# A graph attention layer and a mixture of experts on one core: nodes laid out by partition (p * 48 + t) or by tile (t * 128 + p)

## The chip, the core and the metric

The kernel runs on one core of a Trainium2 chip. The metric is the device time of one execution in microseconds (us). PE is TensorE, DVE is VectorE, ACT is ScalarE, POOL is GpSimd, and SP is the SyncE queue that issues most of the transfers.

## The reference

There are 6250 nodes of 256 numbers (`x`) and a sorted list of 100,000 edges, `src` and `dst`. The first layer needs the first 6250 edges only:

```python
xn = layernorm(x)
xt = (xn @ weight).reshape(-1, 4, 64)
alpha_l = einsum('ehd,hd->eh', xt[src], attn_l)
alpha_r = einsum('ehd,hd->eh', xt[dst], attn_r)
alpha = softmax(leaky_relu(alpha_l + alpha_r, 0.01), axis=1)
tmp = einsum('nh,nhd->nd', alpha[:6250], xt[dst[:6250]])   # node n uses edge n
x = x + broadcast of tmp over the 4 heads
```

The second layer takes the layernorm of x as tokens, routes each to its 2 best of 8 experts, and adds their outputs, weighted, to the token; the sum is added to x:

```python
logits = tokens @ router_w.T;  rw, re = top_k(softmax(logits), 2);  rw = rw / rw.sum()
for e in range(8):
    out = out + combine[:, e:e+1] * (gelu(tokens @ w1[e] + b1[e]) @ w2[e] + b2[e])
```

`src` is uniform over the nodes. `dst` is `6250 * u ** 2` for uniform u, truncated to an integer and sorted, so the first 6250 edges name only the lowest-numbered nodes.

## The kernel before

The nodes fill 49 tiles of 128 lanes. Node t * 128 + p lies in tile t on partition p; tile 48 holds the last 106. The program sets the order of every engine's instructions by hand (`manual_schedule`, L133), so an engine takes its instructions in the order in which they are written, and one that waits holds up what stands behind it.

**Loads and lists (L185 to L232).** The edge lists come as rows, 49 x 128, by SP: 48 whole rows, then the last row of 106 (L194, L195). Between the two lists stands the load of the first four tiles of x (L197), after them the other loads of x, up to four tiles each (L206), and the last tile in two pieces (L208). ACT's queue brings the weights, the router and the attention vectors (L198 to L201). The dst list is cast, transposed on PE and cast back to integers (L229 to L232), so that `dst_sb[p, t]` is the edge's target of node t * 128 + p.

**Own terms (L667 to L684).** For each group of up to four tiles of x, PE transposes them (`turn`, L240; ACT copies the result out of PSUM), forms the attention and router terms (`own_terms`, L417, into `own_T`), and turns them back (`back`, L430). DVE takes the mean and variance of 12 or 13 tiles at a time (`statistics`, L402) and scales the terms (`source_end`, L440). Other work is put between these steps by number (`fillers`, L649). Just ahead of this part the src list is split into its low 7 bits (the partition) and the rest (the tile) by DVE (L336 to L350): the partition numbers go through a DRAM tile `highs` to all partitions as `high_1` (L352, L353), which a filler turns into a one-hot table (L655); the tile numbers go through PE to `low`, from which a filler makes `low_0` (L652).

**Gathers (L234, L643).** POOL gathers the rows x[dst] for each tile by an indirect transfer. A small copy on POOL (`pace`, L645) ties the start of every second gather to the progress of the own terms and, later, of the features. A gather is asked for 20 tiles ahead of its use. The 31 middle tiles go to `big`, which later holds the experts' second weights, the other 18 to `xd_own`.

**Features (L755 to L780).** For each gathered tile PE turns it, multiplies with `w_sb` (`features`, L464), and looks up the source terms by matmuls with the two tables (`look_up`, L489); DVE reduces these (L505). Interleaved with the next group of tiles are softmax and weighted sum (`attend_1` to `attend_3`) and routing (`route`, L559), which writes the rows of its group, R = 337 numbers each, to the DRAM table (L593).

**Sorting by expert pair (L783 to L903).** Each token's place among the tokens of its pair of experts is counted by matmuls (`rank`, L605), and a matrix product (L856) gives for each slice and lane the partition and the tile of the token that goes there (`pi`). `held_by` (L901) is its row in the table, and serves as its row of the output too. Then the 125 units (slice and expert) are numbered (L935 to L948), and SP, ACT, PE and DVE load these numbers to registers (`name_units`, loads at L1051).

**Experts (L1125 to L1168).** A pipeline runs over the units: SP loads the first weights (`fill`, L1079), PE multiplies (`first`, L1091; `second`, L1107), ACT applies gelu (L1098), DVE accumulates (L1114). POOL fetches the rows of slices through `held_by` (`fetch`, L914), a token norm is worked off in steps (`norm`, L971), `turn_slice` (L1037, L1038) brings the tokens to `tokT`, and POOL scatters finished slices to the output (`finish`, L1118).

Of the kernel before, what the change touches and what calls it, by code (L numbers as in the profile page):

```python
# [9 lines left out]
FP = mybir.dt.float32  # L10
BF = mybir.dt.bfloat16
I32 = mybir.dt.int32
AF = mybir.ActivationFunctionType
ALU = mybir.AluOpType
# [8 lines left out]
def kernel(  # L23
# [33 lines left out]

    nc = tc.nc  # L60
    N, D = x.shape
    H, OC = attn_l.shape
    NE, _, F = w1.shape
    P = 128
    NT = -(-N // P)
    LAST = N - (NT - 1) * P
    GROUPS = [(0, 10), (10, 10), (20, 9), (29, 10), (39, 10)]
    NG = len(GROUPS)
    GT = max(n for _, n in GROUPS)
# [12 lines left out]
    TS = 128  # L82
    NS = -(-N // TS)
# [15 lines left out]
    HUGE = 2.0**127  # L99
    ROOT_D = D**-0.5  # L100
    assert sum(n for _, n in GROUPS) == NT == NS and HD == D and F == D and NE == 8
    assert 96 <= LAST < P

    const = ctx.enter_context(tc.tile_pool(name="const", bufs=1))
    early = ctx.enter_context(ExitStack())
    held = early.enter_context(tc.tile_pool(name="held", bufs=1))
    ps = ctx.enter_context(tc.tile_pool(name="ps", bufs=2, space=PSUM))
# [20 lines left out]
    number = const.tile([128, 1], FP, name="number")  # L128
    ident = const.tile([128, 128], FP, name="ident")
    ident_b = const.tile([128, 128], BF, name="ident_b")  # L130
    held_by = const.tile([TS, NS], I32, name="held_by")

    dst_sb = held.tile([P, NT], I32, name="dst_sb")  # L133
    xs = [held.tile([P, n, R], FP, name=f"x{g}") for g, (_, n) in enumerate(GROUPS)]
# [39 lines left out]
    small = early.enter_context(tc.tile_pool(name="small", bufs=2))  # L174
# [6 lines left out]
    first_pool = setup.enter_context(tc.tile_pool(name="setup", bufs=1))  # L181
    raw = first_pool.tile([128, DC, HD], FP, name="raw")
    rows = first_pool.tile([NE, D], FP, name="rows")
    att = first_pool.tile([2 * H, OC], FP, name="att")
    edges = [first_pool.tile([NT, P], I32, name=name) for name in ("dst_rows", "src_rows")]  # L185
    whole = (NT - 1) * P
    for of in edges:
        nc.vector.memset(of, 0)

    g_last, n_last = GROUPS[-1]  # L190
    nc.vector.memset(xs[-1][96:, n_last - 1, :D], 0.0)
    x_v = x[0:whole, :].rearrange("(t p) d -> p t d", p=P)
    for of, e in zip(edges, (dst, src)):
        nc.sync.dma_start(of[: NT - 1, :], e[0:whole].rearrange("(t p) -> t p", p=P))  # L194
        nc.sync.dma_start(of[NT - 1 :, :LAST], e[whole:N].rearrange("(t p) -> t p", t=1))  # L195
        if e is dst:
            nc.sync.dma_start(xs[0][:, :4, :D], x_v[:, :4, :])  # L197
    nc.scalar.dma_start(raw, weight.rearrange("(c p) f -> p c f", p=128))  # L198
    nc.scalar.dma_start(rows, router_w)
    for k, a in enumerate((attn_r, attn_l)):  # L200
        nc.scalar.dma_start(att[k * H : (k + 1) * H, :], a)  # L201
    for g, (t0, n) in enumerate(GROUPS):
        for k in range(0, n, 4):
            m = min(4, NT - 1 - t0 - k, n - k)
            if m > 0 and t0 + k > 0:
                nc.sync.dma_start(xs[g][:, k : k + m, :D], x_v[:, t0 + k : t0 + k + m, :])  # L206
# [4 lines left out]
    for of, pattern, k in ((count_up, [[1, 128]], 0), (number, [[0, 1]], 1)):  # L211
        nc.gpsimd.iota(
            of, pattern=pattern, base=0, channel_multiplier=k,
# [9 lines left out]
    nc.vector.memset(counts[:, 0, :], 0.0)  # L223
    nc.vector.tensor_scalar(ident, count_up, number, None, ALU.is_equal)
    nc.vector.tensor_copy(ident_b, ident)


    edge_f = first_pool.tile([NT, P], FP, name="edge_f", bufs=2)
    nc.vector.tensor_copy(edge_f, edges[0])  # L229
    pe = ps.tile([P, NT], FP, name="pe", tag="r")  # L230
    nc.tensor.transpose(pe, edge_f, ident[:NT, :NT])
    nc.vector.tensor_copy(dst_sb, pe)  # L232

    def gather(t):  # L234
        nc.gpsimd.indirect_dma_start(  # L235
# [97 lines left out]
        nc.vector.tensor_copy(w_sb[:, c, AR:MEAN], pa[:, 0, :])  # L333


    parts = []  # L336
    for k, (op, by) in enumerate(
        ((ALU.bitwise_and, P - 1), (ALU.logical_shift_right, P.bit_length() - 1))
    ):
        part = edges[0] if k else first_pool.tile([NT, P], I32, name="src_part")  # L340
        nc.vector.tensor_scalar(part, edges[1], by, None, op)
        parts.append(part)
    high_b = first_pool.tile([NT, P], BF, name="high_b")
    nc.vector.tensor_copy(high_b, parts[0])
    low_f = first_pool.tile([NT, P], FP, name="edge_f", bufs=2)
    nc.vector.tensor_copy(low_f, parts[1])
    pe = ps.tile([P, NT], FP, name="pe", tag="r")
    nc.tensor.transpose(pe, low_f, ident[:NT, :NT])
    low = first_pool.tile([P, NT], BF, name="low")
    nc.vector.tensor_copy(low, pe)  # L350
    highs = dram.tile([1, NT * P], BF, name="highs")
    nc.sync.dma_start(highs.rearrange("o (t p) -> (o t) p", p=P), high_b)  # L352
    nc.sync.dma_start(high_1[:, : NT * P], highs.to_broadcast([P, NT * P]))  # L353
# [199 lines left out]


    table = dram.tile([NT * P, R], FP, name="table")
    table_v = table.rearrange("(t p) r -> p t r", p=P)
    ranks = {}

    def route(g):  # L559
# [195 lines left out]
    at = {}  # L755
    for k, (g, b, n) in enumerate(FEATURES):
        if b == 0:
            at = tasks(g)
        after = None
        for j in range(n):  # L760
            i = b + j
            features(g, i, blocks, j)
            t = GROUPS[g][0] + i
# [20 lines left out]
    n = GROUPS[z][1]  # L784
# [40 lines left out]
    parts = []  # L825
    for k, (op, by) in enumerate(
# [4 lines left out]
        part = small.tile([P, NTE], BF, name=f"part{k}", bufs=1)  # L831
# [11 lines left out]
    for t0, t1 in ((0, 10), (10, 24), (24, NTE)):  # L843
        at, n = slice(t0, t1), t1 - t0
# [16 lines left out]
    for k in range(2):  # L861
# [34 lines left out]
    nc.vector.tensor_tensor(  # L896
        is_unit, long(count_up[:NS, :NU], NE), wide(unit, NU), ALU.is_equal
    )
    tile_of = small.tile([TS, NS], FP, name="tile_of", bufs=1)
    nc.vector.tensor_copy(tile_of, pi[:, 1, :])  # L900
    nc.vector.scalar_tensor_tensor(  # L901
        held_by, tile_of, float(P), pi[:, 0, :], op0=ALU.mult, op1=ALU.add
    )  # L903

    xrs, toks, norms, w1s, hids = ({} for _ in range(5))

# [42 lines left out]

    early.close()
    late = ctx.enter_context(tc.tile_pool(name="late", bufs=3))
    tokT = late.tile([128, NS * D], FP, name="tokT", bufs=1)
# [161 lines left out]
    def finish(s):  # L1116
        n = min(TS, N - s * TS)
        nc.gpsimd.indirect_dma_start(  # L1118
            out=ends_at[s][:, :],
            out_offset=bass.IndirectOffsetOnAxis(ap=held_by[:n, s : s + 1], axis=0),  # L1120
            in_=acc[:n, s * D : (s + 1) * D], in_offset=None,
        )

# [76 lines left out]
```

## Time and profile before

| | us |
|---|---|
| runs of the kernel: median of 3 (lowest, highest) | 430.03 (427.4, 430.1) |
| the profiled execution, its own time | 440.06 |
| its span, first to last instruction | 438.3 |
| PE busy | 376.8 (86%) |
| DVE busy | 311.0 (71%) |
| ACT busy | 225.1 (51%) |
| POOL busy | 201.3 (46%) |

Starts and durations below count from the start of the span of that one profiled execution. A timeline line gives start, duration (of all instructions merged in it), engine, line, operation, out<-in, shape and count, and in brackets the idle time of the engine before it and what ended that. A line of stages gives the stretch, its length, then busy time and count for PE, PE's weight loads, DVE, ACT and POOL, then the granted clock of PE as a share of full speed, the busy share of the 16 DMA engines (over 1 where packets of several queues overlap), and what they moved in GB/s.

### The profile page before, as it was taken

The numbers are of one execution on the slowest core, as the hardware profiler recorded it, in microseconds if no ns is written. First come the engines' busy times: TensorE is split into PE (matmuls) and PEld (weight loads), VectorE is DVE, ScalarE is ACT, GpSimd is POOL, SyncE is SP. The second block draws the span as 40 slices with busy tenths as digits, with TensorE's granted clock in tenths as the row PEclk, the third lists the DMA queues.
The fourth block names the chain that finished last, engine by engine and source line by source line (L and its number), as shares of the span: only waits on it lengthen the run. The fifth ranks groups of instructions, "written<-read, shape, count | busy, mean of one in ns | idle before, by whom it ended". The sixth has DMA issues, their size and how long they took to land.

```text
span 438.3 us, 9881 instructions
## 1 busy us (share of the span) xinstructions
PE 376.8 (86%) x2576; PEld 322.4 (74%) x2576; DVE 311.0 (71%) x1083; ACT 225.1 (51%) x658; POOL 201.3 (46%) x240
## 2 busy tenths in 40 slices
PE   5977979998995018879999999999999999999991
PEld 4745757776884016459999998988988899999990
DVE  5979412989879987548789778777876877655551
ACT  3654457866773100057676666566576577333330
POOL 0077868889222000563443467555665643322222
PEclk9896889999998555699999999999999999999997
DMA  7979544473971340396656676767776666666620
GB/s 239 352 212 84 103 76 80 78 222 117 273 234 59 138 157 0 88 278 167 203 166 203 191 213 203 233 198 207 204 215 201 199 183 192 182 187 196 182 72 22
DMA packets 59109, 74.63 MB, mean 170 GB/s; under 512 B 7171, under 2 KB 54103, under 8 KB 58801
## 3 DMA queue, kind: packets, MB, share of 16 engines
q1 hardware_dynamic: 51504, 52.45, 40.0%
q0 software_dynamic: 7248, 21.29, 20.0%
q8 instruction: 23, 0.38, 0.4%
q10 hardware_dynamic: 304, 0.27, 0.2%
q14 instruction: 30, 0.24, 0.2%
HBM read 59.13 MB, written 14.87 MB: 169 GB/s over the span
## 4 chain that ended last, share of the span: by engine, by line
PE 52%; issue 1%; POOL 1%; ACT 1%; POOLq 0%; ACTq 0%; DVE 0%
PE ph L1091 25%; PE py L1107 24%; PE pt L1037 2%; POOL xr L914 0%; POOLq L1195 0%; ACT tokT L1038 0%; ACT acc L1014 0%; POOL out_dram L1118 0%; ACT tok L1004 0%; POOL nm L994 0%; ACT hid L1098 0%; ACTq L1051 0%; POOL mv L993 0%; ACTq L1098 0%; ACT nm L1010 0%
## 5 line engine op out<-in xcount | busy, mean ns | idle before, releaser
L1091 PEld LDWEIGHTS ph<-tokT,w 128*128 128x128 f32 x1000 | 129.7, 191 | 17.5 <-ACT tokT L1038 5.6
L1091 PE MATMUL ph<-tokT,w 128*128 (+1 forms) x1000 | 133.3, 276 | 5.9 <-ACT tokT L1038 3.3
L1107 PE MATMUL py<-big,hid 128*128 x500 | 128.9, 381 | 0.0
L1098 ACT ACTIVATE hid<-ph,b_cols 128x128 f32<-128x128 f32 x250 | 78.4, 366 | 82.7 <-PE ph L1091 67.2
L1107 PEld LDWEIGHTS py<-big,hid 128*128 128x128 f32 x500 | 85.4, 191 | 7.4 <-DVE acc L1114 0.6
L1114 DVE SCALAR_TENSOR_TENSOR acc<-py,shares,acc 128x256 f32 (+1 forms) x125 | 60.5, 484 | 32.4 <-PE py L1107 15.0
L914 POOL DMA_INDIRECT xr<-table,held_by x49 | 49.3, 1006 | 72.2 <-DVE held_by L901 39.1
L1118 POOL DMA_INDIRECT out_dram<-acc,held_by x49 | 50.9, 1040 | 55.0 <-DVE acc L1114 39.6
L1114 DVE SCALAR_TENSOR_TENSOR acc<-big,shares,acc (+1 forms) x125 | 60.1, 481 | 10.5 <-issue 5.0
L468 PE MATMUL px<-w_sb,tT 128*128 128x293 f32 x196 | 57.4, 423 | 3.8 <-issue 3.3
L1004 ACT ACTIVATE tok<-xr,nm 128x256 f32<-128x256 f32 x49 | 29.5, 603 | 57.2 <-DVE nm L1000 41.1
L468 PEld LDWEIGHTS px<-w_sb,tT 128*128 128x128 f32 x196 | 34.7, 193 | 12.1 <-issue 3.9
L235 POOL DMA_INDIRECT big<-in_x_dram,dst_sb x31 | 34.9, 1126 | 8.1 <-issue 7.4
L250 ACT COPY tT<-pt 128x512 f32<-128x512 f32 (+2 forms) x56 | 27.5, 528 | 13.9 <-PE pt L246 10.5
L476 ACT COPY pxs<-px 128x293 f32<-128x293 f32 x49 | 19.7, 402 | 27.5 <-PE px L468 15.0
L978 DVE TENSOR_TENSOR xr<-xr 128x512 f32<-128x512 f32 (+1 forms) x25 | 17.3, 692 | 17.3 <-issue 17.2
L1014 ACT ACTIVATE acc<-xr,nm 128x256 f32<-128x256 f32 x49 | 29.1, 597 | 0.0
L505 DVE TENSOR_REDUCE ag<-pl 128x8 f32<-128x392 f32 (+1 forms) x25 | 13.8, 551 | 19.3 <-PE pl L501 7.6
L993 POOL TENSOR_SCALAR mv<-mv 128x2 f32<-128x2 f32 (+1 forms) x25 | 5.6, 226 | 38.6 <-DVE mv L990 34.4
L235 POOL DMA_INDIRECT xd_own<-in_x_dram,dst_sb x18 | 19.3, 1073 | 4.9 <-issue 4.1
L246 PE MATMUL pt<-ident,x 128*128 128x128 f32 x98 | 17.1, 324 | 3.8 <-issue 2.0
L497 PE MATMUL pl<-al_sb,high 128*128 128x196 bf16 x147 | 18.6, 246 | 1.8 <-DVE ag L505 1.8
(210 smaller groups left out, 481.3 us busy)
## 6 DMA issues: line engine op xcount, KB each, us to landing
w<-in_L_ffn_w_dram SPq DMA_DIRECT2D x125, 256.0 KB
table<-x SPq DMA_DIRECT2D x4, 1685.0 KB
x<-in_x_dram SPq DMA_DIRECT2D x10, 512.0 KB
big<-in_L_ffn_w_dram SPq DMA_DIRECT2D x2, 1024.0 KB
high<-highs SPq DMA_DIRECT2D x1, 1568.0 KB
table<-x SPq DMA_DIRECT2D x1, 1516.5 KB
big<-in_L_ffn_b_dram SPq DMA_DIRECT2D x1, 1024.0 KB
xr<-table,held_by POOLq DMA_INDIRECT x49
```

The costliest lines, as they stand in the source:

```text
L235: nc.gpsimd.indirect_dma_start(out=xd(t), out_offset=None, in_=x[:, :], in_offset=bass.IndirectOffsetOnAxis(ap=dst_sb[:, t : t + 1], axis=0),)
L250: nc.scalar.copy(tT, pt)
L468: nc.tensor.matmul(px, blocks[c][:, k * P : (k + 1) * P], w_sb[:, c, :], start=(c == 0), stop=(c == DC - 1),)
L476: nc.scalar.copy(pxs[:, i, :], px)
L914: nc.gpsimd.indirect_dma_start(out=xr[:, i, :], out_offset=None, in_=table[:, :], in_offset=bass.IndirectOffsetOnAxis(ap=held_by[:, s0 + i ...
L1004: nc.scalar.activation(tok[:, i, :], xr[:, i, :D], AF.Identity, bias=bias[:, i : i + 1], scale=scale[:, i : i + 1],)
L1014: nc.scalar.activation(acc[:, s * D : (s + 1) * D], xr[:, i, :D], AF.Identity, bias=bias[:, i : i + 1], scale=more[:, i : i + 1],)
L1091: nc.tensor.matmul(ph[:, j, :], w[:, c * F + j * 128 : c * F + (j + 1) * 128], tokT[:, bass.ds(rows_at + c * TS, TS)], start=(c == 0), sto ...
L1098: nc.scalar.activation(hid[:, j, :], ph[:, j, :], AF.Gelu, bias=b1_cols[:, :, j][:, bass.ds(at_act[u][0], 1)])
L1107: nc.tensor.matmul(py, hid[:, j, :], we2[:, j, bass.ds(at_pe[u][1], D)], start=(j == 0), stop=(j == FC - 1),)
L1114: nc.vector.scalar_tensor_tensor(to, y, share, to, op0=ALU.mult, op1=ALU.add)
L1118: nc.gpsimd.indirect_dma_start(out=ends_at[s][:, :], out_offset=bass.IndirectOffsetOnAxis(ap=held_by[:n, s : s + 1], axis=0), in_=acc[:n, ...
```

## The change

With PER = 48 and `whole` = 48 * 128 = 6144, node p * 48 + t (t below 48) lies in tile t on partition p, so that 48 neighbours in x share a partition; the last 106 nodes are tile 48, node `whole` + p on partition p, as before. A load of four tiles of x then takes four consecutive rows for each partition. The table is laid out likewise, row p * 49 + t. The edge lists are loaded straight to their partitions, 48 numbers each; the last 106 edges come as a column by two small loads for each list on ACT's queue. The transposes of the dst list and of the low part of src go. In their place the src list is divided by 48 on DVE (shift by 4, times 171, shift by 9), the remainder and the exception of the last 106 nodes are worked out, and the partition numbers are transposed on PE. As the rows of the table and of the output are no longer numbered alike, `held_out` is worked out by four operations of DVE, called between the unit numbers and the experts.

```diff
-    LAST = N - (NT - 1) * P
+    PER = NT - 1
+    whole = PER * P
+    LAST = N - whole
...
+    held_out = const.tile([TS, NS], I32, name="held_out")
...
-    edges = [first_pool.tile([NT, P], I32, name=name) for name in ("dst_rows", "src_rows")]
-    whole = (NT - 1) * P
-    for of in edges:
-        nc.vector.memset(of, 0)
+    src_sb = first_pool.tile([P, NT], I32, name="src_sb")
+    for of in (dst_sb, src_sb):
+        nc.vector.memset(of[96:, PER:], 0)
...
-    x_v = x[0:whole, :].rearrange("(t p) d -> p t d", p=P)
-    for of, e in zip(edges, (dst, src)):
-        nc.sync.dma_start(of[: NT - 1, :], e[0:whole].rearrange("(t p) -> t p", p=P))
-        nc.sync.dma_start(of[NT - 1 :, :LAST], e[whole:N].rearrange("(t p) -> t p", t=1))
+    x_v = x[0:whole, :].rearrange("(p t) d -> p t d", t=PER)
+    for of, e in ((dst_sb, dst), (src_sb, src)):
+        nc.sync.dma_start(of[:, :PER], e[0:whole].rearrange("(p t) -> p t", t=PER))
         if e is dst:
             nc.sync.dma_start(xs[0][:, :4, :D], x_v[:, :4, :])
...
+    for of, e in ((dst_sb, dst), (src_sb, src)):
+        for p0, p1 in ((0, 96), (96, LAST)):
+            nc.scalar.dma_start(
+                of[p0:p1, PER:], e[whole + p0 : whole + p1].rearrange("(p o) -> p o", o=1)
+            )
...
-    edge_f = first_pool.tile([NT, P], FP, name="edge_f", bufs=2)
-    nc.vector.tensor_copy(edge_f, edges[0])
-    pe = ps.tile([P, NT], FP, name="pe", tag="r")
-    nc.tensor.transpose(pe, edge_f, ident[:NT, :NT])
-    nc.vector.tensor_copy(dst_sb, pe)
...
-    parts = []
-    for k, (op, by) in enumerate(
-        ((ALU.bitwise_and, P - 1), (ALU.logical_shift_right, P.bit_length() - 1))
-    ):
-        part = edges[0] if k else first_pool.tile([NT, P], I32, name="src_part")
-        nc.vector.tensor_scalar(part, edges[1], by, None, op)
-        parts.append(part)
+    src_f = first_pool.tile([P, NT], FP, name="src_f")
+    nc.vector.tensor_copy(src_f, src_sb)
+    nc.vector.tensor_scalar(src_sb, src_sb, 4, None, ALU.logical_shift_right)
+    nc.vector.tensor_scalar(src_sb, src_sb, 171, None, ALU.mult)
+    nc.vector.tensor_scalar(src_sb, src_sb, 9, None, ALU.logical_shift_right)
+    hi = first_pool.tile([P, NT], FP, name="hi")
+    nc.vector.tensor_copy(hi, src_sb)
+    lo = first_pool.tile([P, NT], FP, name="lo")
+    nc.vector.scalar_tensor_tensor(
+        lo, hi, -float(PER), src_f, op0=ALU.mult, op1=ALU.add
+    )
+    over = first_pool.tile([P, NT], FP, name="over")
+    nc.vector.tensor_scalar(over, src_f, float(whole), None, ALU.is_ge)
+    low = first_pool.tile([P, NT], BF, name="low")
+    nc.vector.scalar_tensor_tensor(
+        low, over, float(PER), lo, op0=ALU.mult, op1=ALU.max
+    )
+    nc.vector.scalar_tensor_tensor(
+        src_f, src_f, -float(whole), hi, op0=ALU.add, op1=ALU.subtract
+    )
+    nc.vector.tensor_tensor(src_f, src_f, over, ALU.mult)
+    nc.vector.tensor_tensor(hi, hi, src_f, ALU.add)
+    pe = ps.tile([NT, P], FP, name="pe", tag="r")
+    nc.tensor.transpose(pe, hi, ident)
     high_b = first_pool.tile([NT, P], BF, name="high_b")
-    nc.vector.tensor_copy(high_b, parts[0])
-    low_f = first_pool.tile([NT, P], FP, name="edge_f", bufs=2)
-    nc.vector.tensor_copy(low_f, parts[1])
-    pe = ps.tile([P, NT], FP, name="pe", tag="r")
-    nc.tensor.transpose(pe, low_f, ident[:NT, :NT])
-    low = first_pool.tile([P, NT], BF, name="low")
-    nc.vector.tensor_copy(low, pe)
+    nc.vector.tensor_copy(high_b, pe)
...
-    table_v = table.rearrange("(t p) r -> p t r", p=P)
+    table_v = table.rearrange("(p t) r -> p t r", t=NT)
...
-    tile_of = small.tile([TS, NS], FP, name="tile_of", bufs=1)
-    nc.vector.tensor_copy(tile_of, pi[:, 1, :])
+    part_of = small.tile([TS, NS], FP, name="part_of", bufs=1)
+    nc.vector.tensor_copy(part_of, pi[:, 0, :])
     nc.vector.scalar_tensor_tensor(
-        held_by, tile_of, float(P), pi[:, 0, :], op0=ALU.mult, op1=ALU.add
+        held_by, part_of, float(NT), pi[:, 1, :], op0=ALU.mult, op1=ALU.add
     )
+
+    def rows_of_output():
+        at, more = (small.tile([TS, NS], FP, name=name, bufs=1) for name in ("at", "more"))
+        nc.vector.scalar_tensor_tensor(
+            at, part_of, float(PER), pi[:, 1, :], op0=ALU.mult, op1=ALU.add
+        )
+        nc.vector.tensor_scalar(
+            more, part_of, 1.0 - PER, float(whole - PER), ALU.mult, ALU.add
+        )
+        nc.vector.scalar_tensor_tensor(
+            more, pi[:, 1, :], float(PER), more, op0=ALU.is_equal, op1=ALU.mult
+        )
+        nc.vector.tensor_tensor(held_out, at, more, ALU.add)
...
+    rows_of_output()
     early.close()
...
-            out_offset=bass.IndirectOffsetOnAxis(ap=held_by[:n, s : s + 1], axis=0),
+            out_offset=bass.IndirectOffsetOnAxis(ap=held_out[:n, s : s + 1], axis=0),
```

More of the change, by code (lines that the diff above doesn't have):

```diff
@@ L101 @@
     assert sum(n for _, n in GROUPS) == NT == NS and HD == D and F == D and NE == 8
-    assert 96 <= LAST < P
+    assert 96 <= LAST < P and PER == 48
     const = ctx.enter_context(tc.tile_pool(name="const", bufs=1))
```

## The prediction

> **What bounds the kernel now.** I read the page's slices first, then the busy time by stage, then the timeline of the stages that the diff touches, and last the list of waits.
>
> ```profile
> PE   5977979998995018879999999999999999999991
> DVE  5979412989879987548789778777876877655551
> DMA  7979544473971340396656676767776666666620
> ```
>
> Each digit is 11 us. From slice 18 (198 us) to the end PE is at nine tenths: the expert part, 240 of the profiled 438.3 us. The page's chain says the same (PE 52% of the span, all of it expert matmuls and their transposes). Its order of units is fixed: 125 units whatever the routing, and renaming nodes leaves the number of tokens of each expert pair as it is. So the change can move only what lies ahead of 198 us, by stage:
>
> ```profile
> 12.00:18.00 6.00, 6.00 (x61) 4.77 (x61) 5.89 (x28) 3.44 (x8) 0.00 (x0) 0.72 1.09 351
> 35.00:40.00 5.00, 4.83 (x36) 3.58 (x32) 4.90 (x18) 2.93 (x8) 3.51 (x6) 0.50 1.04 80
> 60.00:72.00 12.00, 11.92 (x76) 9.50 (x75) 2.14 (x4) 7.49 (x23) 8.56 (x12) 0.97 0.44 86
> 108.00:120.00 12.00, 12.00 (x80) 9.77 (x78) 9.95 (x26) 7.96 (x26) 4.10 (x2) 1.00 1.08 275
> 137.00:178.00 41.00, 13.57 (x80) 9.86 (x78) 34.34 (x96) 1.72 (x3) 2.13 (x2) 0.53 0.25 84
> ```
>
> Columns: stretch, its length, then busy us of PE, weight loads, DVE, ACT and POOL, granted clock, share of the DMA engines, GB/s. DVE is full from 12 to 22 and from 29 to 50 us (statistics, attention terms), PE from 60 to 137 (features), DVE from 137 to 178 (routing). DMA is full for the loads of x (to 22.5 us), but nothing in the list of waits above 0.9 us in the first 48 us names x: only the first transposes wait for it, 0.3 us. So a faster x has little to give, and a longer DVE chain is paid at once.
>
> **The loads of x.** Fourteen loads of up to 512 KB leave SP from 3.77 to 17.56 us; their contiguous pieces grow from 1 KB to 4 KB. The row: 351 GB/s at a DMA share of 1.09. The Trainium skill ("DMA: Bandwidth & Descriptors", Specifications) puts line rate at pieces of 512 B and up and the limit of HBM per core near 358 GB/s: both say that 1 KB pieces already run at the limit. By the row 6.3 MB take 18 us before and after; by the page's limit the whole gain is 2%, 0.4 us. I take 0. The cover, should they be slower: statistics of the last 13 tiles start at 35.8 us, 13 us after they have landed.
>
> **The start.** The dst list no longer passes PE: an int cast (0.22), a transpose (0.34) and a cast back (0.21) go, with DVE's wait of 1.53 us for the list at 3.96. SP loses two tail issues (0.32 and 0.23 us) and one of them ahead of the first x tiles, issued at 1.86. These tiles and the weight sum (PE 4.50 to 6.57) gate PE's turn at 6.15. I take 0.5 us earlier (0.3 to 0.7, the issue removed and a memset that gated SP's first issue). Four 4-byte-wide tail loads join ACT's queue, 0.3 to 0.6 us each by the four issues there: about 1.7 us, ahead of the table load (2.50, 1.28 us). ACT's next work starts at 7.46, so they end near 5.5 in its shadow; without it they would cost 1.7. Their data are needed by the src chain at 11 us and the last gather. Gathers start at 21.8.
>
> **The src chain**, the largest cost. Before:
>
> ```profile
> 11.11 0.21 DVE L341 TENSOR_SCALAR src_part<-src_rows 49x128 int32<-49x128 int32 x1
> 11.24 0.21 DVE L341 TENSOR_SCALAR dst_rows<-src_rows 49x128 int32<-49x128 int32 x1
> 11.37 0.21 DVE L344 CAST high_b<-src_part 49x128 bf16<-49x128 int32 x1
> 11.51 0.21 DVE L346 CAST edge_f<-dst_rows 49x128 f32<-49x128 int32 x1
> 11.77 0.13 PEld L348 LDWEIGHTS pe<-ident,edge_f 49*128 49x128 f32 x1 [0.95 <-DVE edge_f L346]
> 11.96 0.86 PEld L246 LDWEIGHTS pt<-ident,x 128*128 128x128 f32 x8
> 12.07 0.21 DVE L350 CAST low<-pe 128x49 bf16<-128x49 f32 x1 [0.35 <-PE pe L348]
> 12.20 4.01 DVE L406 BATCH_NORM_STATS2 stats<-x 128x6 f32<-128x256 f32 x12
> ...
> 34.62 0.19 DVE L452 CAST al_sb<-al_f 128x48 bf16<-128x48 f32 x1
> 34.84 0.21 DVE L454 TENSOR_TENSOR al_f<-al_f,al_sb 128x48 f32<-128x48 f32 x1
> 35.08 0.19 DVE L452 CAST al_sb<-al_f 128x48 bf16<-128x48 f32 x1
> ```
>
> Four independent operations start 0.135 us apart, PE turns the result, DVE casts it, and the statistics follow. Dividing by 48 in place of a shift by 7 takes eleven operations of 128x49 on DVE before PE can turn `hi`. The last three lines show dependent ones of this size 0.24 us apart. Three of the ten steps are independent, seven dependent: 3 x 0.14 + 7 x 0.24 + 0.21 for the last = 2.3 us, against 0.61 (11.11 to 11.72). `low` needs no PE now; its place after the transpose is taken by `high_b`. So PE's transpose, the turn of the next x tiles behind it, and DVE's statistics all come 1.7 us later, less the 0.5 above: **1.2 us**.
>
> Who waits: DVE works nearly without pause to 50 us (except gaps of 1.9 us in all between 22.7 and 26.2), so its last attention terms come at 51.0 rather than 49.8. The first look-up on PE starts at 50.65; 0.85 us of slack, so at least 0.35 passes. The other way to it, through ACT's `own_T`, POOL's `pace` and the gathers, starts from the same turned tiles and would move by up to 1.2. I take 1.0 (0.3 to 1.7): the features then keep PE full, and the shift reaches 178 us. The `highs` store leaves SP at 18.55, after the x loads, 5 us behind a `high_b` at 13.5: hidden.
>
> **Table and gathers.** Five table writes of 1.7 MB keep their places; their rows join to pieces of 13.5 KB. The last leaves at 154.2 and is read from 178.4: 24 us for 1.7 MB, hidden; 0. The 49 gathers of x keep 128 rows each and POOL's 0.95 us; 0 (-5 in the rival below). The row fetches and the output scatter keep sizes and counts; 0 (up to +5 below).
>
> **The tail.** `held_by` keeps its two operations. Four more (`at`, `more` twice, `held_out`) stand on DVE after the unit numbers and ahead of the clearing of `shares`:
>
> ```profile
> 181.34 0.30 DVE L945 SCALAR_TENSOR_TENSOR for_dve<-which 1x125 int32<-1x125 f32 x1
> 181.66 0.43 DVE L957 MEMSET shares<- 128x441 f32 x1
> 183.61 0.43 DVE L978 TENSOR_TENSOR xr<-xr 128x256 f32<-128x256 f32 x1 [1.53 <-issue]
> 187.93 1.16 PE L1091 MATMUL ph<-tokT,w 128*128 128x128 f32 x8 [0.46 <-ACT tokT L1038]
> 189.32 1.16 PE L1091 MATMUL ph<-tokT,w 128*128 128x128 f32 x8 [0.23 <-DMA w<-in_L_ffn_w_dram]
> ```
>
> 0.14 + 2 x 0.24 + 0.21 = 0.8 us (by the 128x49 rows above). Behind them wait the clearing, the register loads (DVE idle 1.53 to 183.61) and the first token norm, which the first expert matmul waits for. The second unit waits 0.2 us for its weights anyway, so **0.6 us** pass (0 if the row fetch, not DVE, ends the wait before 183.61; at most 0.8).
>
> **Sum:** 1.0 + 0.6 = 1.6 us on the profiled execution's 440.06 us (span 438.3 and what lies around it): 441.7. That execution is 10 us above the median of 430.03; the added operations are not among its unexplained gaps, so I add the same us: 431.6.
>
> **Rivals.** *Slower by pitch.* Each x load now takes 4 KB from every 48 KB. The same page (Latency and other measured facts) tells of copies whose rows lie a large power of two apart: 207 GB/s at 512 KiB, 164 at 2 MiB. 48 KB is none, and no run here shows it; against that stands the 351 of a pitch of 1 KB within a tile and 128 KB between tiles. The one gives 6.3 MB in 18 us, the other 38. `high` (1.6 MB, 27 to 32 us) queues behind, and DVE uses it at 43.48: 11 us of slack, so it decides below 6.3 MB in 29 us, 217 GB/s. At 164 the loss is 20 - 11 = 9 us: 440. Chance 0.08.
>
> *Slower in the expert part.* Lanes of one fetch now lie some 28 x 49 rows apart in the table, not 28. PE's waits for `tokT` there are 5.6 us in 7. If 24 pairs of fetches cost 0.2 us more each on that way, +4.8: 436.4. Against it: no neighbouring rows were read before either. Chance 0.14, with other losses of that size.
>
> *Faster by the gathers.* dst is sorted, and by its law (6250 u squared, 100,000 edges) some 1265 edges name node 0: ten columns of 128. In 35 to 40 us, when these gathers are in flight, DMA is full at 80 GB/s; in 60 to 72, 0.44 for 86. Now each gather names some 25 rows. If the crowded queue is also what holds ACT from 52.57 to 57.31 and DVE for 1.9 us near 24, at most 4.7 + 1.9 - 1.6 = 5 us come back: 425.0. Against it: POOL issues one gather in 1.3 us and each tile is asked for 20 tiles ahead, so no gather is waited for; and gaps of a profiled execution need not be in the timed ones. Chance 0.13.
>
> *Hidden anyway.* Only 0.35 of the start passes and the row fetch covers the tail: 430.4. Chance 0.10.
>
> **How the numbers follow.** The likeliest case has 0.55: 431.6, its own range 429.5 to 434. About 1%, 4.3 us, is what a measurement of this kernel can tell from no change. Within 1% are this case and the hidden one: 0.65. Faster 0.13, slower 0.08 + 0.14 = 0.22. The range 425 to 436 leaves out the pitch case, about half of the other slow case and half of the fast one: 0.2.
>
> **What would show it.** Right: statistics starting near 13.4 us rather than 12.20; x loads still ended at about 22 us near 350 GB/s; first look-up near 51.5; four 128x49 operations on DVE ahead of the clearing of `shares`; an expert part of 240 us. Wrong: x waited for in the first 48 us, the first look-up earlier than 50, or an expert part longer or shorter by over 2 us.

## The result and the profile after

| us | before | after |
|---|---|---|
| median of 12 runs each, same chip (lowest, highest) | 428.17 (427.4, 430.25) | 432.0 (431.17, 432.71) |
| ratio of after to before, 95% interval | | 1.0079 (1.0062 to 1.0097) |
| the profiled execution of after, its span | | 431.44, 429.7 |

By the ratio the change costs 3.4 us, 0.8% (the medians lie 3.8 us apart; the runs of before spread over 2.9 us). It lies within the 1% that the prediction called no change, and yet its interval is well clear of 1: a small loss, not none. In a later set of runs the medians were 432.57 and 428.01 and the ratio 1.0097 (1.0072 to 1.0123), 4.2 us.

The profile that the prediction reads took 440.06 us, which is the level of one chip of a later set (median of 43 runs of the kernel before: 440.06); in three other sets of runs it takes 428.0 to 428.5. Below, "the 440 level" and "the 428 level" mean these. The absolute times of that first profile must therefore not be laid against those of after; its stretches of a few us can.

The page of after, its slices (tenths busy, 10.7 us each):

```profile
PE   5796799888993117969999999999999999999991
DVE  5999525897988897548778878877876877555551
DMA  7974232456663120665767676777777665666620
```

PE is again at nine tenths from 193 us (18 slices in) to the end, so the bound is the same. The new thing stands in the DMA row: its fourth to eighth slices are 4 2 3 2 4, where before had 9 5 4 4 4.

The stages of after (columns as before: busy us of PE, weight loads, DVE, ACT, POOL, granted clock, DMA share, GB/s):

```profile
12.00:18.00 6.00, 5.03 (x37) 3.95 (x38) 5.36 (x24) 2.03 (x4) 0.00 (x0) 0.50 1.09 359
35.00:40.00 5.00, 3.79 (x51) 2.52 (x49) 4.92 (x18) 1.87 (x8) 4.17 (x6) 1.00 0.34 107
60.00:72.00 12.00, 12.00 (x76) 9.70 (x75) 3.71 (x13) 9.84 (x28) 10.31 (x14) 1.00 0.27 83
108.00:120.00 12.00, 12.00 (x87) 10.01 (x85) 11.12 (x32) 8.68 (x26) 2.24 (x2) 1.00 0.68 235
137.00:178.00 41.00, 17.89 (x92) 11.46 (x90) 32.18 (x86) 1.61 (x3) 4.49 (x5) 0.50 0.22 85
```

The loads of x still move 359 GB/s at a share of 1.09. Between 35 and 40 us the DMA engines moved 107 GB/s at a share of 0.34, where before had 80 at 1.04: gathers of many different rows keep the DMA engines busy for less of the time. DVE is full in the same stages as before.

The start of after, from the timeline:

```profile
10.49 0.16 DVE L333 COPY own<-pa 128x4 f32<-128x4 f32 x1 [0.21 <-PE pa L329]
...
10.64 0.18 DVE L338 CAST src_f<-src_sb 128x49 f32<-128x49 int32 x1
10.85 0.19 DVE L339 TENSOR_SCALAR src_sb<-src_sb 128x49 int32<-128x49 int32 x1
...
12.71 0.21 DVE L358 TENSOR_TENSOR hi<-hi,src_f 128x49 f32<-128x49 f32 x1
...
12.97 0.45 PE L360 MATMUL pe<-ident,hi 128*49 128x128 f32 x1 [2.52 <-DVE hi L358]
...
13.46 0.28 DVE L362 CAST high_b<-pe 49x128 bf16<-49x128 f32 x1 [0.54 <-PE pe L360]
13.67 4.00 DVE L418 BATCH_NORM_STATS2 stats<-x 128x6 f32<-128x256 f32 x12
```

Eleven operations run from 10.64 to 12.92, PE waits 2.52 us for the last of them, DVE waits 0.54 for PE, and the statistics, 12.20 in the prediction's lines, start at 13.67. PE's own part of it grew too: it now turns 128 columns, where before it turned 49 in

```profile
11.78 0.26 PE L348 MATMUL pe<-ident,edge_f 49*128 49x49 f32 x1 [0.85 <-DVE edge_f L346]
```

The tail of after, the same view:

```profile
174.95 0.95 POOL L939 DMA_INDIRECT xr<-table,held_by  x1 [0.30 <-issue]
...
175.25 0.30 DVE L970 SCALAR_TENSOR_TENSOR for_dve<-which 1x125 int32<-1x125 f32 x1
175.45 0.19 DVE L919 SCALAR_TENSOR_TENSOR at<-part_of,pi 128x49 f32<-128x49 f32 x1
175.56 0.34 DVE L922 TENSOR_SCALAR more<-part_of 128x49 f32<-128x49 f32 x1
...
176.19 0.26 DVE L928 TENSOR_TENSOR held_out<-at,more 128x49 int32<-128x49 f32 x1
...
176.81 0.43 DVE L983 MEMSET shares<- 128x441 f32 x1 [0.36 <-DMA xr<-table,held_by]
...
178.68 0.43 DVE L1004 TENSOR_TENSOR xr<-xr 128x256 f32<-128x256 f32 x1 [1.44 <-issue]
...
182.99 2.05 PE L1117 MATMUL ph<-tokT,w 128*128 128x128 f32 x16 [0.46 <-ACT tokT L1064]
```

From the last unit number (L970) to the clearing of `shares` there are 1.56 us (175.25 to 176.81), against 0.32 before. The sixteen matmuls of the first two units stand in one line, without a wait for weights between them.

**Where the 3.4 us lie.** Executions of one kernel differ by about 2 us in their first stages (see the end), so traces of the same kind of start must be compared. Of the same kind as the profiled after, at the same 428 level (but in another set of runs) and with the old order of nodes, is the kernel with spread gathers below (428.11 us), whose gathers turn out to move no time:

| us from the start of the span | old order, spread gathers | after | difference added |
|---|---|---|---|
| first statistics on DVE | 12.1 | 13.7 | +1.6 |
| `held_by` on DVE | 170.0 | 171.8 | +0.2 |
| first expert matmul | 180.2 | 183.0 | +1.0 |
| last issue of an output scatter | 417.9 | 421.3 | +0.6 |
| end of the span | 426.3 | 429.7 | 0.0 |

So two places hold 2.6 of the 3.4 us; the 0.6 of the expert part is taken up again under the rivals' last point. Theory: two chains of small DVE operations, each put where the next thing waits for DVE. Rivals: the pitch of the x loads, the gathers, the scattered rows in the expert part.

### The profile page after: what moved, and what is told of

Same layout as the page of the kernel before. It is cut to its first block, busy times and chain, and to the rows that moved or that the text cites. A ratio compares the mean times of both kernels' runs of the same rounds, so it can differ in the third digit from the quotient of the medians.

```text
span 429.7 us, 9894 instructions
## 1 busy us (share of the span) xinstructions
PE 369.3 (86%) x2575; PEld 320.6 (75%) x2575; DVE 312.8 (73%) x1092; ACT 226.7 (53%) x658; POOL 200.1 (47%) x240
## 4 chain that ended last, share of the span: by engine, by line
PE 46%; POOL 2%; issue 2%; DVE 2%; ACT 1%; POOLq 0%; ACTq 0%; DVEq 0%
PE ph L1117 23%; PE py L1133 21%; PE pt L1063 2%; DVE acc L1140 1%; POOL xr L939 1%; POOL nm L1020 1%; ACT hid L1124 1%; DVE stats L1014 0%; POOLq L1221 0%; ACT acc L1040 0%; DVEq L1077 0%; ACT tokT L1064 0%; POOL mv L1019 0%; ACTq L1077 0%; POOL out_dram L1144 0%
## 5 line engine op out<-in xcount | busy, mean ns | idle before, releaser
L1144 POOL DMA_INDIRECT out_dram<-acc,held_out x49 | 50.9, 1039 | 55.4 <-DVE acc L1140 39.2
L1140 DVE SCALAR_TENSOR_TENSOR acc<-big,shares,acc (+1 forms) x125 | 60.2, 481 | 11.3 <-issue 6.1
L236 POOL DMA_INDIRECT big<-in_x_dram,dst_sb x31 | 33.8, 1090 | 7.2 <-issue 5.5
L1004 DVE TENSOR_TENSOR xr<-xr 128x512 f32<-128x512 f32 (+1 forms) x25 | 17.2, 688 | 17.0 <-issue 17.0
L517 DVE TENSOR_REDUCE ag<-pl 128x8 f32<-128x392 f32 (+1 forms) x25 | 13.8, 552 | 12.1 <-PE pl L513 12.1
L1020 POOL TENSOR_TENSOR nm<-mv,half_c 128x2 f32<-128x2 f32 (+1 forms) x25 | 18.3, 734 | 2.1
```

The lines of the kernel that those rows point to most:

```text
L236: nc.gpsimd.indirect_dma_start(out=xd(t), out_offset=None, in_=x[:, :], in_offset=bass.IndirectOffsetOnAxis(ap=dst_sb[:, t : t + 1], axis=0),)
L1020: nc.gpsimd.tensor_tensor(scale, mv[:, :n, 1], half_c[:, :n], ALU.pow)
L1140: nc.vector.scalar_tensor_tensor(to, y, share, to, op0=ALU.mult, op1=ALU.add)
L1144: nc.gpsimd.indirect_dma_start(out=ends_at[s][:, :], out_offset=bass.IndirectOffsetOnAxis(ap=held_out[:n, s : s + 1], axis=0), in_=acc[:n, ...
```

## The experiments

**Which gaps belong to the kernel.** The kernel before, profiled once on each of two chips.

> The kernel before, unchanged, profiled once more, since its first profiled execution took 440.06 us against a median of 428.17 and shows gaps that nothing explains. Expected: about 428 us, statistics from 12.2 us, first pace copy on POOL at 21.4, and 9.9 us from the end of held_by to the first expert matmul. Theory (the PE wait for hi and the four operations of the tail): the first look-up some 2 us earlier than the 50.55 of the changed kernel. Rival (expert part slower with scattered rows): the first look-up at about the same time, and the expert part 2 to 3 us shorter than in the changed kernel.

> The kernel before, profiled on the chip of this set, as the trace to lay beside the others. On a chip of the 428 level: statistics from 11.9 us, held_by near 169.8, last output transfer issued near 418. On one of the 440 level: as the first two traces of this kernel.

Measured 441.29 us (span 439.5) on the chip of the 440 level and 429.93 us (span 428.2) on one of the 428 level. The first missed the expected 428 by 13 us. DVE's gaps near 24 us came again on the first (0.66, 0.66 and 0.65 us) and not on the second. ACT's 4.7 us at 52.57 came on neither in that size (1.85 us at 54.5 on the first; nothing above 1.33 us between 50 and 60 on the second). At the 428 level the "4.7 + 1.9" of the rival by the gathers was nothing to win.

**Moving the two added waits.** Three kernels move work of after without taking any away: one calls `rows_of_output` right behind `held_by`, where DVE waits for PE anyway; one puts the transpose of `hi` and the stores of `highs` behind the first own terms, so that the statistics follow DVE's chain at once; one does both.

```diff
+    rows_of_output()
...
-    rows_of_output()
...
-    nc.tensor.transpose(pe, hi, ident)
...
+    def src_turned():
...
+        if k == 0:
+            src_turned()
```

> The changed kernel with the four operations for held_out moved right behind held_by, where DVE stands idle for 1.57 us before the unit numbers. Theory: 1.1 us less than the changed kernel's 432.0, so 430.9, and 9.9 us from held_by to the first expert matmul. Rival (the loss lies in the expert part or in the transfers): within 0.3 us of 432.0.

> The changed kernel with the transpose of hi, high_b and the two transfers of highs moved behind the first own terms, so that PE goes on to turn x instead of waiting for the eleven operations of DVE. Theory: PE turns the second tiles at about 10.6 us in place of 13.2, POOL's first pace copy comes at about 21 in place of 23.5, and 2.1 us are saved: about 429.9. If DVE's statistics are what counts (they start some 0.6 us earlier only), 0.6 us: 431.4. Rival (loss elsewhere): 432.0.

> Both moves. Theory: 3.2 us less than the changed kernel, 428.8 us, that is equal to the kernel before within 1 us either way. Rival (expert part or transfers slower by the new order of rows): 431 or more.

All three ran on the chip of the 440 level: 444.15 us, 1.0088 (1.0063 to 1.0113), six runs; 441.38, 1.0027 (1.0013 to 1.0042); 441.38, 1.0027 (1.0012 to 1.0042). In the traces the first of them brings the way from `held_by` to the first expert matmul back from 11.2 to 10.1 us, as meant, but the totals do not show it: the tail moved alone is no better than after, and added to the other it gains nothing. On this chip the runs of one kernel lie up to 7 us apart (before: 438.64 to 445.37), and after itself was not run there. The totals are inconclusive, so after and the kernel with both moves were run again on a chip of the 428 level.

> The changed kernel once more, beside the three others of this set on one chip, since the level of the kernel before differs by 12 us between chips (428 and 440). Expected 1.0079 times the kernel before, as on the first chip. If the losses of the start and the tail add up on any chip, the ratio holds within 0.002; if a chip's own gaps take up a part of them, it is smaller where the level is 440.

> Both moves once more (the transpose of hi behind the first own terms; held_out right behind held_by). Theory: equal to the kernel before within 0.2%, and 0.5 to 0.8% faster than the changed kernel of this set. Rival (transfers, gathers, scattered rows cost by themselves): slower than before by 0.3% or more, as 1.0027 on the chip of the last set suggests.

432.57 and 430.67 us, 1.0097 (1.0072 to 1.0123) and 1.0049 (1.0032 to 1.0066): both moves bring 1.9 us back. But equality with before was expected, and the 0.3% that spoke for the rival is passed: 2.1 us of loss remain. The timeline of the kernel with both moves, start and tail:

```profile
11.32 0.16 DVE L333 COPY own<-pa 128x4 f32<-128x4 f32 x1 [0.62 <-PE pa L329]
...
13.54 0.21 DVE L358 TENSOR_TENSOR hi<-hi,src_f 128x49 f32<-128x49 f32 x1
13.67 1.73 DVE L419 BATCH_NORM_STATS2 stats<-x 128x6 f32<-128x256 f32 x5
...
172.38 0.18 DVE L925 TENSOR_SCALAR more<-part_of 128x49 f32<-128x49 f32 x1
...
173.91 0.47 DVE L966 TENSOR_SCALAR which<-pf 1x125 f32<-1x125 f32 x2 [0.86 <-PE pf L959]
...
175.60 0.30 DVE L975 SCALAR_TENSOR_TENSOR for_dve<-which 1x125 int32<-1x125 f32 x1
175.93 0.43 DVE L987 MEMSET shares<- 128x441 f32 x1
```

From the last copy of `own` to the statistics 2.35 us go by, 3.18 in after: 0.83 less. `more` takes 0.18 in place of 0.34, DVE still waits 0.86 for `pf` behind the four operations, and the clearing follows the unit numbers after 0.33: the tail is 10.1 us again, 1.1 less than in after. 0.83 + 1.1 = 1.9, what the runs gave. Of the 2.1 us that remain, 1.0 is the chain itself: it still stands ahead of the statistics, whose way is 2.35 us here and 1.31 in the kernel before (below). For the other 1.1 no place was found. The version at the end of this part keeps the new order of rows and is faster than before, so that order as such does not cost them.

**Adding each chain to the kernel before.** Four dependent 49x128 operations go ahead of PE's transpose at the start, or four like those of `rows_of_output` ahead of the clearing of `shares`.

```diff
+    for _ in range(4):
+        nc.vector.tensor_scalar(low_f, low_f, 1.0, None, ALU.mult)
     pe = ps.tile([P, NT], FP, name="pe", tag="r")
```

```diff
...
+    nc.vector.scalar_tensor_tensor(at, tile_of, 1.0, pi[:, 0, :], op0=ALU.mult, op1=ALU.add)
+    nc.vector.tensor_scalar(more, tile_of, 1.0, 0.0, ALU.mult, ALU.add)
+    nc.vector.scalar_tensor_tensor(more, pi[:, 0, :], 1.0, more, op0=ALU.mult, op1=ALU.mult)
+    nc.vector.tensor_tensor(spare, at, more, ALU.add)
```

> The kernel before with four more dependent operations of 49x128 on DVE (times 1) ahead of the transpose of the tile numbers on PE: the changed kernel's wait on PE, and nothing else of the change. They put the transpose near 12.9 us, where the changed kernel has it, in place of 11.77. Theory: 1.1 us of chain and 0.9 us of PE work at half clock behind it, 2 us slower in all (0.47%). Rival (PE's wait is absorbed by POOL's gathers later): under 0.5 us.

> The kernel before with four operations of 128x49 on DVE between the unit numbers and the clearing of shares, results unused: the tail of the changed kernel alone. Theory: the first expert matmul 1.1 us later after held_by, and 1.1 us slower in all (0.26%). Rival (the expert part takes it up, since its first units wait for weights anyway): under 0.4 us.

The first: 430.15 us, 1.0039 (1.0021 to 1.0057), 1.7 us more. Its timeline:

```profile
12.20 0.21 DVE L346 CAST edge_f<-dst_rows 49x128 f32<-49x128 int32 x1
12.44 0.98 DVE L348 TENSOR_SCALAR edge_f<-edge_f 49x128 f32<-49x128 f32 x4
...
13.98 1.39 DVE L408 BATCH_NORM_STATS2 stats<-x 128x6 f32<-128x256 f32 x4
```

Four operations take 0.98 us, 0.245 each, and the way from the last copy of `own` (11.65) to the statistics is 2.33 us, against 1.31 in the profile of before at the 428 level (11.80 to 13.11). Nothing up to `held_by` takes this 1.0 us back: from the statistics to `held_by` 157.8 us go by here and 157.8 to 157.9 in three kernels of the old order (those with spread gathers, with the loads of x changed and with the tail added). The 1.7 timed contain the 1.0 within their interval (0.9 to 2.4), and PE's wait is not absorbed.

The second: 431.75 us, 1.0069 (1.0047 to 1.0092), 3.0 us more. Its timeline:

```profile
172.94 0.95 POOL L914 DMA_INDIRECT xr<-table,held_by  x1 [0.30 <-issue]
...
173.55 0.34 DVE L954 TENSOR_SCALAR more<-tile_of 128x49 f32<-128x49 f32 x1
...
174.79 0.43 DVE L963 MEMSET shares<- 128x441 f32 x1 [0.36 <-DMA xr<-table,held_by]
```

Here too `more` takes 0.34 us and the clearing waits 0.36; from `held_by` to the first expert matmul 11.2 us go by, against 10.1 to 10.2 without the four: +1.0 to 1.1 without any change of layout, as in after. Laid beside the second profile of after, of the same chip and the same kind of start and with the same four operations in its tail, only the start is left: the first statistics are 1.9 us later in after, `held_by` 1.8, the first expert matmul 1.8, the last issue of an output scatter 1.9. The timed loss is larger than the trace's, and above the 1.1 expected. Its runs lie in two groups, four from 429.25 to 429.81 and eight from 430.66 to 432.78, and the profiled one is of the lower; why more of them than usual lie in the upper is not known.

**The rivals.** First the kernel before with the new pitch of its x loads alone (each x tile then holds other rows than its node numbers say):

```diff
-    x_v = x[0:whole, :].rearrange("(t p) d -> p t d", p=P)
+    x_v = x[0:whole, :].rearrange("(p t) d -> p t d", t=NT - 1)
```

> The kernel before with the loads of x alone changed (each partition takes consecutive rows, 48 KB apart between partitions), and nothing else: it adds the wrong rows of x to the tokens, and only its time counts. Theory: no difference, within 0.2%, the loads ended at 22 to 23 us near 350 GB/s. Rival of the pitch: the loads below 217 GB/s and over 1% slower.

428.95 us, 0.9998 (0.9981 to 1.0016). The same stage of this kernel:

```profile
12.00:18.00 6.00, 5.21 (x50) 4.01 (x51) 5.57 (x31) 2.43 (x6) 0.00 (x0) 1.00 1.09 353
```

Rows 48 KB apart move 353 GB/s, those of the kernel before 354 (below, at the 428 level). Neither the rival by the pitch nor a gain by larger pieces is there. Then the kernel before with gathers of 128 different rows (of nodes other than the edges'):

```diff
+    nc.gpsimd.iota(spread, pattern=[[127, NT]], base=0, channel_multiplier=1)
...
-            in_offset=bass.IndirectOffsetOnAxis(ap=dst_sb[:, t : t + 1], axis=0),
+            in_offset=bass.IndirectOffsetOnAxis(ap=spread[:, t : t + 1], axis=0),
```

> The kernel before with its 49 gathers taking 128 different rows each (row 127 t + p) in place of the few rows that dst names: it gathers the wrong nodes, and only its time counts. Theory: the DMA share from 48 to 84 us falls (from about 0.45 to 0.3, as in the changed kernel), and the time stays within 0.2%, since no gather is waited for. Rival (crowded rows hold up the start): 1 to 5 us faster.

428.39 us, 0.9993 (0.9976 to 1.0011). Its stages, and then those of the kernel before at the 428 level:

```profile
35.00:40.00 5.00, 2.60 (x31) 1.77 (x30) 5.00 (x25) 1.85 (x6) 4.08 (x6) 0.94 0.35 103
...
60.00:72.00 12.00, 12.00 (x75) 9.49 (x74) 5.82 (x16) 10.34 (x30) 10.18 (x13) 1.00 0.25 70
```

```profile
12.00:18.00 6.00, 5.39 (x49) 4.19 (x49) 5.54 (x31) 2.43 (x5) 0.00 (x0) 1.00 1.09 354
...
35.00:40.00 5.00, 3.38 (x39) 2.19 (x33) 5.00 (x26) 1.88 (x7) 4.08 (x7) 1.00 0.91 84
...
60.00:72.00 12.00, 12.00 (x80) 9.86 (x78) 3.17 (x11) 9.84 (x26) 10.09 (x14) 1.00 0.37 83
```

Crowded rows do keep the DMA engines busy, 0.91 in place of 0.35 between 35 and 40 us, and after has the low shares too. But POOL is busy 4.08 us of 5 either way and PE full from 60 us: no gather is waited for, and nothing is won. The prediction's rival by the gathers (425.0 us) is out.

**A version that keeps the new layout.** DVE has idle time between its operations at the start: while it waits for `pr` and for `pa`. Eleven operations of the src chain go there, the src list is loaded ahead of dst, `high_b` follows the first statistics, and `rows_of_output` stands behind `held_by`.

```diff
-    for of, e in ((dst_sb, dst), (src_sb, src)):
+    for of, e in ((src_sb, src), (dst_sb, dst)):
...
+    src_f = first_pool.tile([P, NT], FP, name="src_f")
+    nc.vector.tensor_copy(src_f, src_sb)
...
+        if k == 0:
+            src_out()
...
+    rows_of_output()
```

> The changed kernel with the eleven operations on the src list put into DVE's idle time at the start (five where it waits 1.26 us for the router's transpose, six where it waits 1.21 us for the attention sums), high_b and its transfers behind the first statistics, the column of src loaded ahead of that of dst, and held_out worked out right behind held_by. Theory (DVE is unbroken from the first statistics to the first look-up, so their start sets the time): statistics start at 11.0 to 11.3 us in place of 13.7 and of 11.9 in the kernel before, the tail as before; 0.7 us faster than before (ratio 0.998) and 4 us faster than the changed kernel. If the lists arrive too late for the idle time, 1 us is lost and it equals the kernel before. Rival (transfers or scattered rows cost something by themselves): 1.002 or more.

427.31 us (16 runs), 0.9976 (0.9955 to 0.9998): faster than both kernels, than before by 1.0 us (1.2 by the medians), if only just clear of noise. Its timeline:

```profile
6.58 0.17 DVE L305 CAST src_f<-src_sb 128x49 f32<-128x49 int32 x1
...
8.14 0.17 DVE L311 COPY own<-pr 128x16 f32<-128x16 f32 x1 [0.50 <-PE pr L294]
...
9.80 0.21 DVE L336 TENSOR_TENSOR hi<-hi,src_f 128x49 f32<-128x49 f32 x1
...
11.85 0.16 DVE L356 COPY own<-pa 128x4 f32<-128x4 f32 x1 [0.62 <-PE pa L352]
...
12.00 3.35 DVE L421 BATCH_NORM_STATS2 stats<-x 128x6 f32<-128x256 f32 x10
```

The chain is done at 10.01, and the statistics start 0.15 us after the last copy of `own`. In the kernel before they start 1.24 to 1.31 after it: this version hides the whole of the src chain, also the part that before paid. Its statistics were expected at 11.0 to 11.3; its start is of the slower kind (see the end). It keeps every transfer of the new layout: the pitch of x, the order of the table and the scattered rows of the output. Together these cost too little to eat up what is gained at the start (by the traces 1.1 to 1.3 us: 12.00 against 13.11 and 13.29 in two executions of the old order of the same kind).

## Why the prediction was right, and what was too small

The likeliest case came true: two added costs, no gain from loads or gathers, a loss within 1%. The predicted 431.6 stood on the given median of 430.03, and the 12 runs of before now give 428.17; the sum, not only the level, is what must be held against the runs: 1.6 us predicted, 3.4 measured. That the change still fell within 1% owes something to luck: the sum was less than half of what came.

- **Loads of x, 0.** Right; 353 GB/s and 0.9998 with the loads changed alone. The rule on row pitches of large powers of two (the Trainium skill, "DMA: Bandwidth & Descriptors", Latency and other measured facts) says nothing against 48 KB, and no run here shows a loss.
- **The src chain, 1.7.** 2.28 us by the trace against 2.3 by the step's own sum: right, and so is the 0.24 us for a dependent operation. The step that failed is what stands behind it. It took PE's turn and DVE's cast to be as long as before. From the end of the chain to the statistics 0.75 us go by (12.92 to 13.67), before 0.48 (11.72 to 12.20): PE's turn, now of 128 columns in place of 49, takes 0.45 in place of 0.26 and the cast 0.28 in place of 0.21. That is 0.27 us not in the sum.
- **The start, 0.5 earlier.** The last copy of `own` ends the part that the lighter start speeds up. It is at 10.49 and 10.57 in the two profiles of after, and at 10.96, 10.85 and 10.63 in three executions of the old start of the same kind: 0.28 us by the means, less than the spread of the three.
- **How much passes, 1.0 of 1.2.** 1.67 + 0.27 - 0.28 = 1.66, and the statistics are 1.6 later. All of it passes: `held_by` is 1.8 later. The slack of 0.85 us at the first look-up, read from the profile of the 440 level, was no cover: DVE works without a pause from the statistics to 48 us and carries the shift on. The mark chosen for it, "first look-up near 51.5", was poor: PE's first look-up is at 50.55 in one profile of after and at 49.11 in the other, and between 47.1 and 51.2 in the five executions of the old order at the 428 level. What moves it is told at the end ("An issue held up").
- **The tail, 0.6, at most 0.8.** 1.0 to 1.1. The four operations alone took 1.0 (175.45 to 176.45), and the clearing waited 0.36 more, by the profile for a row fetch; 0.1 came back before L1004. The operations are longer than the rows they were sized by because `more` is: 0.34 us, ending at 175.90, which is when POOL's issue of a row fetch ends (174.95 + 0.95); in the kernel with the four operations added it is 173.89 for both. With no fetch beside it, in the kernel with both moves, it takes 0.18. The Trainium skill ("SBUF — State Buffer", SBUF: two separate sides) names a port pair that VectorE in a two-port mode and GpSimd hold by turns, each for a whole instruction; these lines agree with it in that `more` does not end before the issue, but no trace here shows which mode `more` runs in. The cover of 0.2 us was not there: on a chip of the 428 level the first two units are one stretch of sixteen matmuls in the kernel before too (2.05 us from 182.35). The wait for weights in the prediction's last line is in none of the profiles of that level, and the whole delay passes.
- **Table, gathers and rows of the expert part, 0.** Right for the gathers (0.9993). From the first expert matmul to the last output issue 238.3 us go by in after, against 237.7 in the kernel with spread gathers. Most of this 0.6 goes with the chip: on one chip the old order takes 238.1 and 238.3 (the two kernels with operations added) and the new one 238.4 twice (after and both moves), on another the old order takes 237.4 to 237.7 in three kernels and the version that keeps the new layout 238.0. That leaves 0.1 to 0.6 us for the scattered rows, within what single profiles can tell; the 4.8 us of the rival are out.

Added up: 1.6 + 0.2 + 1.0 + 0.6 = 3.4. The two added costs were the right ones; the start was sized at 1.0 in place of 1.6 and the tail at 0.6 in place of 1.0 to 1.1. At the start PE's longer turn (0.27) was missing and the lighter beginning gave 0.28, not 0.5; in both places the cover taken off was not there. The 0.2 and the 0.6 have no shown cause. Of the rivals, a loss by pitch and a gain by the gathers are out, a loss by scattered rows is at most some tenths of a us, and the costs are not hidden.

## What to carry to other kernels

A small operation costs what its place makes of it: the same eleven operations take 2.3 us of the time ahead of the first statistics and none of it in DVE's waits of the first 10 us, so before a layout is changed, ask where its index arithmetic will stand. When a step is lengthened, cost also the turn to the next engine and back, and what runs beside it: `more` took 0.34 us beside a row fetch and 0.18 without. A cover of a few tenths of a us counts only if what covers does not itself stand still while the covered thing moves.

## What the runs showed of the hardware that was not expected

**Two kinds of start.** The same eight small matmuls (`pa`) take either 0.96 or 1.72 us, in 6 and 8 of the 14 profiled executions. From the timelines of the kernel with spread gathers and of the kernel before at the 428 level:

```profile
9.85 0.96 PE L331 MATMUL pa<-terms,turned 128*128 128x8 f32 x8
...
10.85 0.16 DVE L335 COPY own<-pa 128x4 f32<-128x4 f32 x1 [0.22 <-PE pa L331]
```

```profile
10.04 1.72 PE L328 MATMUL pa<-terms,turned 128*128 128x8 f32 x8
...
11.80 0.16 DVE L332 COPY own<-pa 128x4 f32<-128x4 f32 x1 [0.62 <-PE pa L328]
```

The second kind starts its statistics 1 us later. In the kernel with the loads of x changed, which is of this kind, they are 1.2 us later than in the one with spread gathers, `held_by` is 1.2 and the end 0.9 later. So two single profiles can differ by 1 us and more without any cause in the kernels. Between 13.5 and 15 us the granted clock is 0.50 in five of the six executions of the first kind and 1.00 in all of the second. The Trainium skill ("TensorE: Matmul & The Clock Gate", What's actually happening) tells of a clock that is halved by windows whose phase is not tied to the kernel's start; that could make eight matmuls slow in some executions and later ones in others, but the record has 1.00 while the slow eight run, so the cause stays open.

**Chips differ.** The kernel before takes 428.0 to 428.5 us (medians of three sets of runs) and 440.06 on one other chip, 2.7 to 2.8% more, with gaps there (DVE's near 24 us) that nothing in the profile ends. Why is not known. Times of the two levels cannot be compared; ratios taken on one chip can.

**Crowded rows.** While gathers named one row many times, the DMA engines were busy for 0.91 of the time and moved 84 GB/s; with different rows it was 0.35 for 103. A high DMA share is then no sign that bandwidth is used.

**An issue held up.** In all 14 profiles, what POOL does beside DVE's two table operations (2.6 and 1.8 us) is held up. In the two profiles of after:

```profile
40.87 2.63 DVE L664 TENSOR_TENSOR low<-count_up,low 128x2401 bf16<-128x2401 f32 x1
...
41.38 4.00 POOL L236 DMA_INDIRECT big<-in_x_dram,dst_sb  x1 [0.30 <-ACT tT L251]
...
45.61 0.26 ACT L439 COPY own_T<-pa 32x128 f32<-32x128 f32 x1 [4.39 <-POOL pace L657]
```

```profile
40.80 0.95 POOL L236 DMA_INDIRECT big<-in_x_dram,dst_sb  x1 [0.31 <-ACT tT L251]
...
41.06 2.62 DVE L664 TENSOR_TENSOR low<-count_up,low 128x2401 bf16<-128x2401 f32 x1
...
41.74 1.98 POOL L657 COPY pace<-own_T 128x1 f32<-128x1 f32 x1
...
43.75 0.26 ACT L439 COPY own_T<-pa 32x128 f32<-32x128 f32 x1 [3.11 <-POOL pace L657]
```

In the first, the issue of a gather starts 0.5 us after DVE's first table operation and ends 0.1 us after the second (45.25), in place of 0.98 us. In the second, the issue comes 0.26 us ahead of it and is done in 0.95; then the `pace` copy is held until the first table operation ends (43.68). ACT's last `own_T` waits for `pace`, PE for ACT, and the first look-up comes 1.4 us sooner. The kernel before at the 428 level and the version that keeps the new layout are like the first: an issue of 4.20 us. In these three the granted clock between 48 and 56 us is 0.80 to 0.93, in five others 0.99 to 1.00; and from the first statistics to `held_by` 158.1 us go by in after and 159.2 and 159.0 in the other two, against 157.8 to 157.9 in the five. So it seems that which of two instructions comes first, by some tenths of a us, costs 0.3 to 1.4 us in either layout. This is read from eight profiles; no run tests it.
